# New places for a difference in quarters, for the ends of groups of statistics and for the last outputs

## Chip, cores, metric

One core of one Trainium2 chip. Times are device microseconds of that core, medians over executions. The changed kernel is compared with the kernel before on the same chip.

## The reference

Two layers of a compressed interaction network on x of 4096 rows, 32 fields, 16 numbers each (65536 sites), in float32:

```python
def _batchnorm(h, gamma, beta):
    mean = jnp.mean(h, axis=(0, 2), keepdims=True)
    var = jnp.var(h, axis=(0, 2), keepdims=True)
    return (h - mean) * jax.lax.rsqrt(var + EPS) * gamma[None, :, None] + beta[None, :, None]

def _cin_layer(out, x, W, b, gamma, beta):
    r, _, e = x.shape
    h = jnp.einsum('rne,rfe->rnfe', out, x).reshape(r, -1, e)
    h = jnp.einsum('rce,oc->roe', h, W) + b[None, :, None]
    return _batchnorm(h, gamma, beta)

h1 = _cin_layer(x, x, W1, b1, g1, beta1)             # 128 channels
out, direct1 = (h1[:, :64], h1[:, 64:])
direct2 = _cin_layer(out, x, W2, b2, g2, beta2)      # 64*32 products -> 128 channels
return jnp.concatenate([direct1, direct2], axis=1).sum(axis=-1)
```

## The kernel before

The second layer is 64 chunks of 512 columns. A chunk has four stages k = 0 to 3. In each, ScalarE makes two factors in PSUM, VectorE multiplies them with x into z ("zz", two products of 128x2048), and TensorE multiplies z with the weights. Three of the stages (k = 1, 2, 3) run a Strassen scheme, for which GpSimd adds parts of z into t. While a chunk's products are made, VectorE and ScalarE also put together the sums of the chunk before (`combine`, a generator; each `step()` runs one piece of it). The pieces that the change touches:

```python
def difference(part):                                     # 128x256, both inputs in SBUF
    cols = slice(part * T // 2, (part + 1) * T // 2)
    return nc.vector.tensor_tensor(xs[1][:, cols], xs[1][:, cols], xs[0][:, cols], ALU.subtract)

def combine(c, sums_):                                    # (cut)
    x62, x34, x57, x11 = sums_.banks                      # PSUM
    both = cpool.tile([P, T], FP, tag="both", name="both")
    act(both[low], x11[high])                             # ScalarE
    act(both[high], x11[low], bias=b2[low])
    if idle:
        dve(idle.pop(0))                                  # a quarter of the difference, if one is due
    yield
    add(both, both, x11)                                  # VectorE
    yield
    e = cpool.tile([P, 2, T], FP, tag="e", name="e")
    add(e[:, 0], both, x62)
    yield
    ...                                                   # u2, u3, u3_low, e[:, 1]
    dve(lambda: stats_x.add(c, e[:, 0]))                  # bn_stats; every 16th time also bn_aggr
    dve(lambda: stats_y.add(c, e[:, 1]))
    yield
    dve(lambda: nc.vector.tensor_reduce(d2[:, :, c, :], ..., AX.X, ALU.add))
    yield

for c in range(NC):                                       # (cut)
    ...
    if c % DIFF == 4:                                     # chunks 4, 20, 36
        idle += [lambda k=k: difference(k) for k in range(4)]
    for k, i in enumerate(STAGES):
        multiply(z[:, 0::3], f1, b)
        if k in (1, 2, 3): step()
        f2 = factor(raw[i], i, 1)
        if k == 1: step()
        multiply(z[:, 1:3], f2, bx)
        if k == 1: step()
        if k == 2: step()
        ...
        if k == 0: step(2)
        if k == 1: step()
        ...                                               # matmuls and, for k > 0, GpSimd's additions
```

After the loop: the rest of `combine`, the groups of statistics put together, scale and shift, one scaling each of dx and dy (128x2048), and four output transfers of 512 KB, each from 64 partitions.

## Time and profile before

| | before |
|---|---|
| median, lowest, highest of 4 runs | 2158.41, 2157.66, 2160.82 us |
| span of the profiled run | 2156.4 us |
| first to last matmul of the second layer | 1625.71 us |
| last matmul to the end | 23.12 us |

The last two rows are read from the view of two stretches of the profile. Columns: stretch, its length, busy time of TensorE, of its weight loads, VectorE, ScalarE, GpSimd (with counts), TensorE's clock, share and rate of the transfers.

```profile
507.62:2133.33 1625.71, 1606.69 (x7424) 527.15 (x7424) 1517.76 (x1038) 599.18 (x829) 1326.51 (x384) 1.00 0.70 164
2133.33:2156.45 23.12, 0.00 (x1) 0.00 (x0) 9.09 (x22) 3.51 (x4) 0.00 (x0) 0.61 0.41 91
```

TensorE is without work for about 19 us of the second layer (1625.71 - 1606.69), and for the 23 us behind it. The ends of matmuls are modelled in the profile, so stalls can also hide in TensorE's busy time.

### The profile page before, as it was taken

What the parts mean: (1) busy time and instruction counts of PE and PEld (TensorE: products, weight loads), DVE (VectorE), ACT (ScalarE), POOL (GpSimd) and SP (SyncE); (2) the same over time, 40 slices, a digit from 0 to 9 for tenths busy, and PEclk for the clock granted to TensorE, in tenths of its full rate; (3) what the DMA queues carried; (4) which work ended last, traced back from release to release, by engine and by line L of the source; (5) the groups of instructions that cost most, each with busy time, mean ns of one, the idle gap of its engine ahead of it and who ended that gap; (6) DMA issues with size and microseconds to landing.
All of it is one profiled execution on the core that took longest, in us unless ns stands there. A gap on an engine that the chain in (4) does not pass through costs nothing.

```text
span 2156.4 us, 23381 instructions
## 1 busy us (share of the span) xinstructions
PE 2095.2 (97%) x8716; PEld 732.2 (34%) x8716; DVE 1957.4 (91%) x1434; ACT 854.2 (40%) x1221; POOL 1328.3 (62%) x390
## 2 busy tenths in 40 slices
PE   7999999998999999999999999999999999999995
PEld 3344444443332333333223333332333333333331
DVE  7888889887999999899999999999999999999995
ACT  3455555554333333333333333333433333333332
POOL 0000000003877888877788888877888888788884
PEclk9999999999999999999999999999999999999998
DMA  9999999997767677776677777766676777766751
GB/s 348 343 345 329 338 348 362 344 339 188 173 155 167 169 184 173 174 173 160 156 167 184 167 173 170 179 162 156 157 176 165 173 172 173 167 165 163 172 125 40
DMA packets 111699, 440.64 MB, mean 204 GB/s; under 512 B 13024, under 2 KB 13024, under 8 KB 102880
## 3 DMA queue, kind: packets, MB, share of 16 engines
q1 hardware_dynamic: 104992, 416.33, 72.1%
q10 hardware_dynamic: 6592, 22.81, 2.9%
q8 instruction: 68, 1.11, 0.2%
q14 instruction: 47, 0.39, 0.1%
HBM read 417.07 MB, written 22.02 MB: 204 GB/s over the span
## 4 chain that ended last, share of the span: by engine, by line
PE 80%; POOL 11%; DVE 4%; issue 2%; DMA 2%; ACT 0%; SPq 0%; DVEq 0%; POOLq 0%
PE x L426 60%; PE ps L316 18%; POOL t L445 7%; POOL t L442 4%; DVE zz L401 2%; PE ps L314 1%; DVE z L304 1%; DMA b<-in_xb 1%; DVE e L396 0%; DMA a<-in_xa 0%; DMA x<-in_xb 0%; DMA r<-in_xr 0%; DVE direct L361 0%; DVE s_sb L252 0%; SPq L220 0%
## 5 line engine op out<-in xcount | busy, mean ns | idle before, releaser
L426 PE MATMUL x<-zz,w_sb 128*64 128x512 f32 x2560 | 969.0, 594 | 0.0
L442 POOL TENSOR_TENSOR t<-zz 128x1024 f32<-128x1024 f32 x192 | 456.7, 2378 | 787.2 <-DVE zz L401 787.1
L426 PE MATMUL x<-zz,s_sb 128*64 128x512 f32 x2048 | 924.9, 594 | 4.6 <-issue 4.6
L445 POOL TENSOR_TENSOR t<-zz,t 128x2048 f32<-128x2048 f32 x192 | 875.7, 4561 | 15.1
L426 PE MATMUL x<-t,s_sb 128*64 128x512 f32 x1536 | 700.9, 594 | 19.0 <-POOL t L445 19.0
L393 ACT ACTIVATE f<-a,keep 128x512 f32<-128x512 f32 x512 | 398.2, 778 | 637.9 <-DVE zz L401 635.1
L401 DVE TENSOR_TENSOR zz<-f,b 128x2048 f32<-128x2048 f32 x256 | 582.3, 2274 | 0.9 <-ACT f L393 0.8
L401 DVE TENSOR_TENSOR zz<-f,bx 128x2048 f32<-128x2048 f32 x256 | 582.5, 2275 | 0.0
L316 PE MATMUL ps<-z,w_sb 128*128 128x512 f32 x1024 | 450.5, 598 | 6.2 <-DVE z L304 6.2
L426 PEld LDWEIGHTS x<-zz,s_sb 128*64 128x64 f32 x2048 | 281.3, 137 | 371.9 <-issue 363.0
L426 PEld LDWEIGHTS x<-t,s_sb 128*64 128x64 f32 x1536 | 203.6, 137 | 475.3 <-issue 388.6
L426 PE MATMUL x<-t,w_sb 128*64 128x512 f32 x768 | 364.3, 597 | 0.0
L304 DVE TENSOR_TENSOR z<-a,b 128x2048 f32<-128x2048 f32 x128 | 292.6, 2286 | 58.3 <-DMA b<-in_xb 29.6
L426 PEld LDWEIGHTS x<-zz,w_sb 128*64 128x64 f32 x2560 | 301.6, 137 | 109.6 <-issue 107.6
L316 PEld LDWEIGHTS ps<-z,w_sb 128*128 128x128 f32 x1024 | 192.8, 191 | 262.6 <-issue 240.8
L426 PE MATMUL x<-zz,neg_sb 128*64 128x512 f32 x512 | 230.2, 592 | 0.0
L272 ACT ACTIVATE e<-ps,bn_sb 128x512 f32<-128x512 f32 x127 | 87.3, 687 | 245.2 <-PE ps L316 232.4
L396 DVE TENSOR_TENSOR both<-both,x 128x512 f32<-128x512 f32 x64 | 43.8, 685 | 105.2 <-ACT both L393 105.2
L393 ACT ACTIVATE u<-e,bn_sb 64x512 f32<-64x512 f32 x64 | 46.2, 722 | 216.3 <-DVE e L396 216.3
L426 PEld LDWEIGHTS x<-zz,neg_sb 128*64 128x64 f32 x512 | 70.2, 137 | 146.3 <-issue 146.3
L426 PEld LDWEIGHTS x<-t,w_sb 128*64 128x64 f32 x768 | 98.5, 137 | 0.0
L97 DVE BATCH_NORM_STATS2 stats<-e 128x6 f32<-128x512 f32 x127 | 87.1, 686 | 2.7 <-ACT e L272 2.7
(69 smaller groups left out, 870.5 us busy)
## 6 DMA issues: line engine op xcount, KB each, us to landing
a<-h SPq DMA_DIRECT2D x256, 512.0 KB, 5.5
b<-in_xb SPq DMA_DIRECT2D x128, 512.0 KB, 7.0
a<-in_xa SPq DMA_DIRECT2D x128, 512.0 KB, 5.9
b<-in_xb SPq DMA_DIRECT2D x64, 1024.0 KB, 7.1
bx<-in_xb SPq DMA_DIRECT2D x64, 512.0 KB, 6.1
bx<-x SPq DMA_DIRECT2D x64, 512.0 KB, 7.8
h<-kept ACTq DMA_DIRECT2D x64, 256.0 KB, 5.9
r<-in_xr SPq DMA_DIRECT2D x16, 512.0 KB, 7.5
```

Source lines behind the costliest of these rows:

```text
L97: done = nc.vector.bn_stats(self.stats[:, t % SG, :], h)
L272: nc.scalar.activation(e, ps, AF.Identity, bias=b1)
L304: nc.vector.tensor_tensor(z, a.rearrange("p (a t) -> p a t", a=2).unsqueeze(2).to_broadcast([P, 2, 2, T]), b.rearrange("p (b t) -> p b t", ...
L314: nc.tensor.matmul(ps, w1_sb[rows, 4 + s // 4, :], zr[rows, :], start=True, stop=False)
L316: nc.tensor.matmul(pss[t], w1_sb[:, m, :], z[:, m // 2, m % 2, :], start=False, stop=(m == 3))
L393: return queue("act", lambda: nc.scalar.activation(to, source, AF.Identity, **scale_bias))
L396: return dve(lambda: nc.vector.tensor_tensor(to, x, y, ALU.add))
L401: dve(lambda: nc.vector.tensor_tensor(z, a, b.rearrange("p (k q) t -> p k q t", k=2), ALU.mult))
L426: queue("pe", lambda: nc.tensor.matmul(self.of[x], w, b, start=start, stop=stop))
L442: queue("pool", lambda: nc.gpsimd.tensor_tensor(t2, t3, b11, ALU.add))
L445: queue("pool", lambda: nc.gpsimd.tensor_tensor(t[:, 1:3], z[:, 2:4], twice, ALU.subtract))
```

## The change

Its intent, as its edits show it: no VectorE instruction that could wait for GpSimd stands where GpSimd works. So the quarters move behind the next product, and the ends of the groups (which get two copies and, as groups now differ in size, scalings of the variance) go to the same place. The last group is small (4 in place of 16), so little is left for the end. The outputs are scaled and written in quarters, the first before the last reduction. The core of the diff:

```diff
-SG = 16
+SG = 20
+LAST = 4
@@ class Stats: add() no longer aggregates; instead
+        def aggregate(self):
+            size = self.sizes[self.group]            # 20, 20, 20, 4
+            group = self.groups[:, self.group]
+            stats = self.stats[:, :size].rearrange("p a b -> p (a b)")
+            done = nc.vector.bn_aggr(group[:, 1:3], stats)
+            if size != LAST:
+                done = nc.vector.tensor_scalar(group[:, 2:3], group[:, 2:3], size / LAST, None, ALU.mult)
+            ...
+    def swap_groups():
+        g = stats_x.group
+        stats_x.aggregate()
+        nc.vector.tensor_copy(groups2[low, 1, g], stats_x.groups[high, g])
+        return nc.vector.tensor_copy(groups2[high, 1, g], stats_x.groups[low, g])
@@ combine
-        if idle:
-            dve(idle.pop(0))
         yield
         add(both, both, x11)
         yield
         e = cpool.tile([P, 2, T], FP, tag="e", name="e")
+        if idle:
+            dve(idle.pop(0))
         add(e[:, 0], both, x62)
@@
+        if stats_x.ended():
+            ends = [swap_groups, stats_y.aggregate]
+            if c < NC - 1:
+                idle[:0] = [lambda: [end() for end in ends][-1]]
+            else:
+                for end in ends:
+                    dve(end)
@@ after the loop: the reduction is left for later, then
+    act(dy[:, :part], dy[:, :part], scale=ss2[:, 0:1], bias=ss2[:, 2:3])
+    write(nc.scalar, dy, 0, in_y)
+    scale(dx, 0, swapped)
+    write(nc.sync, dx, 0, in_x)
+    with tc.issue_after(lasts["dve"].ins):
+        step()                                       # the last reduction
+    scale(dx, 1, swapped)
+    write(nc.sync, dx, 1, in_x)
+    scale(dy, 1, ss2)
+    write(nc.scalar, dy, 1, in_y)
```

(Cut: the bookkeeping of groups, and `scale_shift` as a function of its own; the operations in it are the same.)

## The prediction

> **What bounds the kernel now.** I read the page first (busy shares, then the chain that ended last), then the waits, then the timelines of VectorE, GpSimd and TensorE side by side over single chunks.
>
> ```profile
> PE 2095.2 (97%) x8716; PEld 732.2 (34%) x8716; DVE 1957.4 (91%) x1434; ACT 854.2 (40%) x1221; POOL 1328.3 (62%) x390
> ...
> PE 80%; POOL 11%; DVE 4%; issue 2%; DMA 2%; ACT 0%; SPq 0%; DVEq 0%; POOLq 0%
> ```
>
> TensorE is busy 97% of the span and is 80% of the chain. GpSimd, busy only 62%, still holds 11% of the chain: somewhere TensorE waits for it. The kernel has two layers. The first ends near 500 us and the change hardly touches it. The second runs 64 chunks from 507.6 us to 2133.3 us. Each chunk has 7424/64 = 116 matmuls that run in pairs, 58 pairs, and in the timeline of TensorE a pair starts every 0.43 us: 24.85 us a chunk if nothing stalls.
>
> The starts of the addition into "both" (one a chunk, on VectorE) give the real periods. Most alternate between 24.89 and 25.0, mean 24.95. Three groups of chunks do not: periods 26.98, 26.94, 26.96, 26.99, 24.04, 25.84 for chunks 3 to 8, and nearly the same at chunks 19 to 24 and 35 to 40. Against 24.95 a chunk they cost 8.05, 7.98 and 8.04 us, together 24.1 us. These are the chunks in which a quarter of the "difference" stands in VectorE's order.
>
> ```profile
> L160 DVE TENSOR_TENSOR x<-x x16: 418/4146/4177, 70.5 to 1501.8; 128x256 f32<-128x256 f32 x16
> ```
>
> That is minimum, median and maximum in ns: 0.42 us in the first layer, where GpSimd does nothing, and about 4.15 us in the second. The timelines show why (VectorE, then GpSimd, then VectorE in a chunk without it):
>
> ```profile
> 1418.68 2.27 DVE L401 TENSOR_TENSOR zz<-f,bx 128x2048 f32<-128x2048 f32 x1
> 1420.88 4.17 DVE L160 TENSOR_TENSOR x<-x 128x256 f32<-128x256 f32 x1
> 1424.97 0.68 DVE L396 TENSOR_TENSOR both<-both,x 128x512 f32<-128x512 f32 x1
> ```
> ```profile
> 1420.23 4.53 POOL L445 TENSOR_TENSOR t<-zz,t 128x2048 f32<-128x2048 f32 x1
> 1430.78 2.38 POOL L442 TENSOR_TENSOR t<-zz 128x1024 f32<-128x1024 f32 x1 [6.02 <-DVE zz L401]
> ```
> ```profile
> 1373.08 0.69 DVE L396 TENSOR_TENSOR both<-both,x 128x512 f32<-128x512 f32 x1 [2.01 <-ACT both L393]
> ```
>
> The quarter is issued 0.65 us into GpSimd's last L445 of a chunk and ends 0.3 us after it (1420.23 + 4.53 = 1424.76). VectorE would have idled 2.01 us there anyway, waiting for ScalarE's "both"; the other 2.0 us push back both, two products, and so GpSimd's next L442. The waits name the victim: 85.5 us (85 times, some of each a gap that is always there) and 19.0 us of TensorE waiting for GpSimd's L445.
>
> ```profile
> PEld x L426 <- POOL t L445: 85.5, 85, 1.7
> PE x L426 <- POOL t L445: 19.0, 26, 0.8
> ```
>
> **What the Trainium skill says.** "SBUF — State Buffer", section "Who interferes with whom": a VectorE instruction with two SBUF inputs contends with a GpSimd instruction that reads SBUF, and whichever comes second blocks until the other is done. This trace agrees: 4.15 against 0.42 us. The same section says that an instruction with one SBUF input does not contend: the product L401 (its f is in PSUM) takes 2.27 us over a busy and over an idle GpSimd. It also lists copies and tensor_scalar as contending; the trace has one copy of 64x2 (L361) at 4.02 us while GpSimd works, and its twin at 0.17 us. Of transfers, the section "Door 1: The DMA port swizzle" gives a transfer from 64 partitions half the ports, and "Can I just issue two DMAs to hit both halves?" says two of them serialize. The last outputs agree: four transfers of 512 KB, 64 partitions each, have their packets from 2145.3 to 2155.1 us largely one after the other, 2.1 MB in 9.9 us.
>
> **The change part by part.**
>
> (1) The quarters move from before "both" to behind the next stage's first product (L401), before the addition into e. GpSimd is idle there: in the last chunk its L445 ends at 2106.45, that product ends at 2107.45 and the next L442 starts at 2110.39. So 1.0 us of margin before and 2.9 us of idle GpSimd after, and the quarter should take 0.42 us, some 0.34 of it net (neighbours overlap by 0.08). All three groups' 24.1 us of lock wait goes. In its place 0.34 us now lies on the path VectorE to GpSimd's first L442 to TensorE. How much slack has that path? Taking TensorE's first use of L445's result minus L445's end in a chunk without a quarter, from the timelines: about 1.9 us in the second stage, 1.0 in the third, 0.05 in the fourth, as each stage is 6.0 us of TensorE (14 pairs) and 6.95 of GpSimd. So there is none at a chunk's end, and a delay is a stall. But a chunk's L442 is released through both by the previous chunk's x11 sums, which come before the stall. The loop therefore spans two chunks (24.89 + 25.02 = 49.91 us), and of two delays of one size in a row the second falls into the time the first has bought. After a long stall the next chunk indeed shows 0.94 us of slack at its end. Four quarters in a row should cost 2 x 0.34 = 0.7 us.
>
> (2) The ends of a group of statistics. Before: two aggregations of 0.59 us in a stage with slack, and no chunk after one is longer. Now they go into the same slot as the quarters, at chunks 21, 41 and 61. An aggregation of 96 numbers takes 0.588 us and of 24 numbers 0.263, so 4.5 ns a number and 0.70 us for 120. Two of them, two scalings of 0.20 and two copies of 0.19 (durations 0.15 and 0.17 of such rows in the tail, with gaps): 2.2 us less some overlap, say 2.0 us. It is on the path with no slack, so each costs 2.0. At 41 and 61: 4.0. At 21 it stands among the quarters and hides one of them: 20 costs 0.34, 21 raises it to 2.0, 23 adds 0.34: 2.35. The loop: -24.1 + 0.7 + 2.35 + 0.7 + 4.0 = **-16.3 us**.
>
> (3) The tail after TensorE:
>
> ```profile
> 2136.31 0.69 DVE L97 BATCH_NORM_STATS2 statsx<-e 128x6 f32<-128x512 f32 x1
> 2137.04 0.59 DVE L102 BATCH_NORM_AGGREGATE groupsx<-statsx 128x2 f32<-128x96 f32 x1
> ...
> 2138.59 0.59 DVE L102 BATCH_NORM_AGGREGATE groupsy<-statsy 128x2 f32<-128x96 f32 x1
> 2139.10 1.16 DVE L490 TENSOR_REDUCE d<-e 128x64 f32<-128x1024 f32 x1
> 2140.17 0.16 DVE L552 COPY groups<-groupsy 128x12 f32<-128x12 f32 x1
> 2140.36 0.26 DVE L108 BATCH_NORM_AGGREGATE mv<-groups 128x2 f32<-128x24 f32 x1
> ```
>
> Last groups of 4 save 0.32 twice, the reduction behind the first scaling saves 1.08, the copy of y 0.19: mv starts 1.9 us earlier. The first scaling is a half: VectorE's 1.34 us becomes 0.7, so the first output is issued 1.9 + 0.65 = 2.55 us earlier. The second halves are issued about 1.8 us behind the first, while the first 1 MB still has 4.7 us to transfer, so they keep the transfers fed, and the end should move with the first issue: **-2.5 us**. Eight transfers instead of four may give some of it back.
>
> (4) Layer one ends with an aggregation of 24 numbers in place of 96: 0.58 - 0.26 = **-0.3 us**. The other ends there are of VectorE in a stage where transfers run at 99%: nothing. The additional memsets come in the first us.
>
> Sum: -16.3 - 2.5 - 0.3 = -19.1; 2159.06 - 19.1 = 2140.
>
> **The rivals.** (a) The lock moves with the quarter: if GpSimd still works when the slot comes, the wait returns. Against it: 1.0 us of margin. For it: the chunk behind an aggregation, where GpSimd runs 2 us late; there TensorE's own stall in the third stage delays both by about 1 us too, so margin remains. If it came back in a few chunks, 2145. (b) The loop does not forgive: every quarter costs its whole 0.34 us, 4.1 in place of 1.7, and the ends are longer (a copy that slips into GpSimd's time): 2143 to 2148. (c) The opposite: the ends overlap better, or the chunk that follows makes up for a part, as after the old groups (24.04 once): 2134 to 2137. (d) Transfers are the bound of the tail: with packets of 4 KB instead of 8 KB and eight issues the time after the last matmul stays: 2142.
>
> **Range and chances.** The first term is measured and sure, as the quarters can't wait where GpSimd is idle; the terms put in its place are estimates good to 3 us, the tail to 1.5 us, and the runs scatter by 1.5. 2134 to 2146 should hold it 8 times in 10. 2% is 43 us, more than all that the change touches (24 of quarters and 23 of tail): faster 0.02, slower 0.01, same 0.97.
>
> **What would show it.** In the changed profile the second layer's quarters take about 0.42 us, all periods of 27.0 are gone, the three group ends take about 2 us in front of an L401 and each is followed by a chunk period of about 26.9; mv starts some 5 us after the last matmul's end instead of 7.0, and the first output is issued 2.5 us nearer to it. It is wrong if a quarter still takes over 1 us, if the periods with a quarter are over 25.3, or if the time between the last matmul and the end has not shrunk by at least 1 us.

## The result, and the profile after

The changed kernel takes 2138.97 us (4 runs, 2137.44 to 2139.49) against 2158.41 us. The ratio of the fast runs is 0.9907 (95% interval 0.989 to 0.9924). The forecast was 2140 us, within a range of 2134 to 2146 us, and "the same within 2%": all held.

The page of the changed kernel, busy shares and chain:

```profile
PE 2091.2 (98%) x8716; PEld 733.8 (34%) x8716; DVE 1916.1 (90%) x1465; ACT 853.8 (40%) x1221; POOL 1328.5 (62%) x390
...
PE 83%; POOL 8%; DVE 4%; issue 2%; DMA 2%; ACT 1%; SPq 0%; DVEq 0%; POOLq 0%
```

TensorE's and GpSimd's work is what it was; VectorE lost 41 us of "busy" time that was waiting (12 quarters at 3.74 us are 45 us), and gained some instructions. The two stretches again, and the quarters (minimum, median, maximum in ns):

```profile
508.02:2116.86 1608.84, 1602.12 (x7424) 528.62 (x7424) 1475.55 (x1050) 599.46 (x829) 1326.67 (x384) 1.00 0.68 166
2116.86:2135.72 18.86, 0.00 (x0) 0.00 (x0) 9.35 (x23) 2.56 (x4) 0.00 (x0) 0.62 0.39 111
```
```profile
L184 DVE TENSOR_TENSOR x<-x x16: 414/416/424, 71.1 to 1488.2; 128x256 f32<-128x256 f32 x16
```

The second layer is 16.87 us shorter, the tail 4.26 us. No quarter waits any more. TensorE's waits for GpSimd's long addition (L481, formerly L445), of which 85.5 and 19.0 us stood before:

```profile
PEld x L462 <- POOL t L481: 58.5, 74, 1.7
PE x L462 <- POOL t L481: 6.5, 12, 0.8
```

A chunk with a quarter, VectorE first, then GpSimd:

```profile
634.51 2.28 DVE L437 TENSOR_TENSOR zz<-f,b 128x2048 f32<-128x2048 f32 x1
636.71 0.41 DVE L184 TENSOR_TENSOR x<-x 128x256 f32<-128x256 f32 x1
637.04 0.68 DVE L432 TENSOR_TENSOR e<-both,x 128x512 f32<-128x512 f32 x1
```
```profile
631.59 4.55 POOL L481 TENSOR_TENSOR t<-zz,t 128x2048 f32<-128x2048 f32 x1
640.07 2.38 POOL L478 TENSOR_TENSOR t<-zz 128x1024 f32<-128x1024 f32 x1 [3.92 <-DVE zz L437]
```

GpSimd is idle from 636.14 to 640.07, the quarter starts 0.57 us into that. The periods there are 25.35, 24.90, 25.36, 24.89: one delay of 0.34 us per pair of chunks (50.25 against 49.91 us), as forecast.

A group's end, VectorE, chunk 41:

```profile
1538.46 0.69 DVE L120 BATCH_NORM_AGGREGATE groupsx<-statsx 128x2 f32<-128x120 f32 x1
1539.06 0.64 DVE L120 BATCH_NORM_AGGREGATE groups<-statsy 128x2 f32<-128x120 f32 x1
...
1539.81 0.68 DVE L432 TENSOR_TENSOR e<-both,x 128x512 f32<-128x512 f32 x1
1540.52 0.16 DVE L409 COPY groups<-groupsx 64x3 f32<-64x3 f32 x1
...
1540.89 2.29 DVE L437 TENSOR_TENSOR zz<-f,bx 128x2048 f32<-128x2048 f32 x1
```

From the start of "both" (1535.65) to the second product went 5.24 us; without an end it is 3.40 us (1373.08 to 1376.48 before). So an end costs 1.84 us on the path. The two periods behind it are 25.87 and 25.84, 1.80 us above a normal pair.

The tail on VectorE:

```profile
2119.40 0.69 DVE L105 BATCH_NORM_STATS2 statsx<-e 128x6 f32<-128x512 f32 x1
...
2121.53 0.26 DVE L130 BATCH_NORM_AGGREGATE mv<-groups 128x2 f32<-128x24 f32 x1
...
2124.59 1.21 DVE L533 TENSOR_REDUCE d<-e 128x64 f32<-128x1024 f32 x1
```

mv starts 2.13 us behind statsx instead of 4.05, and the reduction stands behind the first scaling.

### The profile page after: what moved, and what is told of

Read it like the earlier page. It is cut to its first block, busy times and chain, and to the rows that moved or that the text cites. A ratio compares the mean times of both kernels' runs of the same rounds, so it can differ in the third digit from the quotient of the medians.

```text
span 2135.7 us, 23411 instructions
## 1 busy us (share of the span) xinstructions
PE 2091.2 (98%) x8716; PEld 733.8 (34%) x8716; DVE 1916.1 (90%) x1465; ACT 853.8 (40%) x1221; POOL 1328.5 (62%) x390
## 4 chain that ended last, share of the span: by engine, by line
PE 83%; POOL 8%; DVE 4%; issue 2%; DMA 2%; ACT 1%; SPq 0%; DVEq 0%; POOLq 0%
PE x L462 63%; PE ps L342 18%; POOL t L481 5%; POOL t L478 3%; DVE zz L437 2%; PE ps L340 1%; DVE z L330 1%; DMA b<-in_xb 1%; ACT both L429 0%; DMA x<-in_xb 0%; DMA a<-in_xa 0%; DMA r<-in_xr 0%; DVE e L432 0%; PE running L358 0%; DVE x L184 0%
## 5 line engine op out<-in xcount | busy, mean ns | idle before, releaser
L481 POOL TENSOR_TENSOR t<-zz,t 128x2048 f32<-128x2048 f32 x192 | 875.8, 4562 | 15.1
L429 ACT ACTIVATE both<-x 64x512 f32<-64x512 f32 x64 | 38.1, 595 | 138.6 <-PE x L462 138.6
```

The costliest lines, as they stand in the source:

```text
L429: return queue("act", lambda: nc.scalar.activation(to, source, AF.Identity, **scale_bias))
L481: queue("pool", lambda: nc.gpsimd.tensor_tensor(t[:, 1:3], z[:, 2:4], twice, ALU.subtract))
```

## The experiments

Ten more kernels ran. The first layer, in which they hardly differ, ends anywhere between 505.3 and 513.5 us in their profiles, and whole times scatter accordingly. The second layer's length scatters little (1608.84, 1608.73 and 1608.79 us in three kernels that differ only in the tail). So small differences are read from the second layer and the tail of the profile, and the times stand beside them.

| kernel | median of its fast runs, us | ratio to before, 95% | second layer, us | tail, us |
|---|---|---|---|---|
| before | 2158.41 | 1 | 1625.71 | 23.12 |
| changed | 2138.97 | 0.9907 (0.989 to 0.9924) | 1608.84 | 18.86 |
| e1 quarters only | 2140.65 | 0.99 (0.9886 to 0.9915) | 1603.95 | 23.11 |
| e2 one input (wrong on purpose) | 2137.4 | 0.9881 (0.9865 to 0.9898) | 1601.90 | 23.15 |
| e3 ends at once | 2141.37 | 0.9904 (0.9888 to 0.9919) | 1614.92 | 19.00 |
| e4 y low first | 2137.49 | 0.9888 (0.9869 to 0.9907) | 1608.73 | 19.03 |
| e5 ends on ScalarE | 2132.55 | 0.9867 (0.9851 to 0.9882) | 1603.83 | 18.94 |
| e6 quarters on GpSimd | 2134.6 | 0.9879 (0.9863 to 0.9896) | 1607.20 | 18.92 |
| e7 product first | 2125.73 | 0.9838 (0.9823 to 0.9852) | 1598.09 | 18.82 |
| e8 all three | 2125.04 | 0.9831 (0.9817 to 0.9846) | 1598.17 | 18.94 |
| e9 quarters late (one run, state unknown) | 2136.27 | none | 1608.79 | 20.30 |
| e10 wide outputs | 2144.93 | 0.9915 (0.9887 to 0.9943) | 1598.13 | 35.64 |

The experiments ran on other occasions than the result, on chip 13 (e1 to e4), 11 (e5 to e8) and 15 (e9, e10). Each ratio is to the kernel before on the same chip, whose medians there were 2162.65, 2160.76 and 2161.99 us. Medians of different groups are therefore not subtracted from each other below; every kernel that ran three rounds is "the same within 2%" as the kernel before.

### e1: the quarters alone

```diff
 # the kernel before
-        if idle:
-            dve(idle.pop(0))
         yield
         add(both, both, x11)
         yield
         e = cpool.tile([P, 2, T], FP, tag="e", name="e")
+        if idle:
+            dve(idle.pop(0))
```

> The kernel before with only the quarters of the difference moved behind the next product. Theory (the quarters waited for GpSimd's reads and pushed its next work back): each of the 12 takes 0.42 us, the three groups of periods of 27 us go (24.1 us), and in their place every second quarter costs 0.34 us, 2.0 us in all: 22 us less, 2136.4 us. Rival 1 (every quarter costs its whole 0.34 us, 4.1 in all): 2138.5. Rival 2 (the change's gain is mainly the tail and the ends): not under 2150.

Measured: 2140.65 against 2162.65 us on that chip, 22.0 us less; the 2136.4 us of the expectation was missed, as it started from the 2158.41 us of the result's own session. The second layer is 21.76 us shorter, each quarter takes 0.41 to 0.43 us, and periods of 25.32 to 25.35 us alternate with short ones. The tail is unchanged. The theory holds at 22 us, rival 2 falls; rival 1 is decided by e2. This one move gains more in the second layer than the whole change (16.87 us): the change gives 4.89 us back there, by the ends of the groups (1608.84 - 1603.95).

### e2: the old place, but one input

```diff
 # the kernel before; wrong result on purpose
-                idle += [lambda k=k: difference(k) for k in range(4)]
+                scrap = const.tile([P, 16], FP, tag="scrap", name="scrap")
+                def one_input(k):
+                    part = xs[1][:, k * 256 : (k + 1) * 256].rearrange("p (r e) -> p r e", e=EMB)
+                    return nc.vector.tensor_reduce(scrap, part, AX.X, ALU.add)
+                idle += [lambda k=k: one_input(k) for k in range(4)]
```

> Wrong result on purpose. The kernel before, and in the old place of the 12 quarters an instruction with one input in SBUF instead of two (a reduction over the same 256 columns). Theory (it is the second SBUF input that waits for GpSimd, not the place): it takes 0.4 us inside the 2 us for which VectorE waits there anyway, no period is over 25.2, and the time is 24 us less, 2134.4. Rival (the place in VectorE's order costs, whatever stands there): periods of 27 us stay, or of 25.3, and 2150 to 2158.

Measured: the second layer is 23.81 us shorter and no period but the very first is over 25.1 us. VectorE's timeline:

```profile
610.08 0.40 DVE L516 TENSOR_REDUCE scrap<-x 128x16 f32<-128x256 f32 x1
612.21 0.69 DVE L396 TENSOR_TENSOR both<-both,x 128x512 f32<-128x512 f32 x1 [1.73 <-ACT both L393]
```

An instruction of the same length and data, in the same place beside a working GpSimd, takes 0.40 us and disappears in the wait for ScalarE. So the place alone isn't what waited, and the second SBUF input is the reading that fits. (The stand-in is also another operation, a reduction with 16 results a row instead of 256; no run separates that.) The difference to e1, 1601.90 against 1603.95 us, is the price of the 12 quarters in their new place: 2.05 us, i.e. 0.34 us for every second one, not 4.1.

### e3: the ends of the groups at once

```diff
 # the changed kernel
-            if c < NC - 1:
-                idle[:0] = [lambda: [end() for end in ends][-1]]
-            else:
-                for end in ends:
-                    dve(end)
+            for end in ends:
+                dve(end)
```

> The changed kernel, with the ends of the statistics' groups where the kernel before had them: at once behind the last statistics, in a stage in which GpSimd works. Theory A (the ends cost their 1.84 us on the path in the slot they were moved to, and would be free in a stage with slack, as the aggregations were before): 5.5 us less than the changed kernel, about 2133.5. Theory B, the change's own reason (the copies and scalings would wait there for GpSimd): a copy or a scaling of more than 2 us in the trace, at chunks 20, 40 and 60, up to 4 us each, 2139 to 2150.

Measured: the second layer is 6.1 us longer than the changed kernel's, 1614.92 us. Theory A falls as stated; the change's own reason is right for the copies. VectorE, then GpSimd:

```profile
1020.79 0.15 DVE L122 TENSOR_SCALAR groupsx<-groupsx 128x1 f32<-128x1 f32 x1
1020.98 1.32 DVE L409 COPY groups<-groupsx 64x3 f32<-64x3 f32 x1
1022.32 0.16 DVE L410 COPY groups<-groupsx 64x3 f32<-64x3 f32 x1
```
```profile
1019.93 2.35 POOL L478 TENSOR_TENSOR t<-zz 128x1024 f32<-128x1024 f32 x1
1022.36 4.56 POOL L481 TENSOR_TENSOR t<-zz,t 128x2048 f32<-128x2048 f32 x1
```

The first copy ends when GpSimd's short addition does (1022.28), 1.16 us later than it need. The second slips between GpSimd's two instructions. It is the same at all three ends: 1.29 to 1.32 us for the first copy, 0.16 us for the second. The scaling of one column did not wait at all. Theory B was mis-sized too: the wait was under the 2 us named. With it the ends took 3.21 us, made GpSimd's next work 2.15 us late, and cost 3.8 to 4.0 us a pair of periods (26.14 + 27.56 at chunk 40, against 49.91).

### e5: the aggregations at once, the rest on ScalarE

```diff
 # the changed kernel (cut)
+            if c < NC - 1:
+                dve(stats_x.aggregate)                    # without the scaling
+                dve(stats_y.aggregate)
         yield                                             # and one step later:
+            for to, source, part in ((low, high, x), (high, low, x)):
+                act(groups2[to, 1, weigh, 0:2], part[source, 0:2])
+                act(groups2[to, 1, weigh, 2:3], part[source, 2:3], scale=SG / LAST)
+            act(y[:, 2:3], y[:, 2:3], scale=SG / LAST)
```

> The changed kernel with the groups' ends taken out of the slot: the two aggregations (one input, which did not wait in the run with the ends at once) stand at once behind the last statistics, where that run had 1.06 us of slack (3.21 us of ends made GpSimd's work 2.15 us late); the scalings and the copies go to ScalarE one step later. Theory (an end costs its 1.84 us in the slot because that slot is on the path; of 1.25 us in the earlier place only 0.2 us are too much): periods over 25.6 are gone, the second layer is 1604 us instead of 1608.8. Rival (the ends' cost is not the place: work on VectorE shows wherever it stands): 1608 to 1609.

Measured: 1603.83 us, 5.0 us less, and no period but the very first over 25.4. So an end's 1.84 us were paid because that slot is on the path: the two aggregations, 1.2 us of VectorE, cost nothing in the earlier place, against the rival. ScalarE takes 0.8 us for the five small pieces, and no period shows them. This is what e1 and the changed kernel together should give: e1's second layer, 1603.95 us, with the changed tail.

### e6: the quarters on GpSimd

```diff
 # the changed kernel
-idle += [lambda k=k: difference(k) for k in range(4)]                             # nc.vector
+pool_idle.extend(lambda k=k: difference(k, nc.gpsimd) for k in range(4))          # same slot, GpSimd's queue
```

> The changed kernel with the 12 quarters of the difference computed by GpSimd itself, first thing in its idle stretch of 3.9 us, instead of VectorE. Theory (the quarters' 0.34 us on VectorE are on the path, at 2.05 us in all): 0.6 to 1.2 us each on GpSimd, hidden; the periods of 25.3 at chunks 4, 6, 23, 36, 38 are gone and the second layer is 1606.8 us. Rival (GpSimd is the scarcer engine there, or VectorE and GpSimd block each other again): at or above 1608.8.

Measured: 1607.20 us, 1.6 us less, about as expected (1606.8). The rows of that difference on GpSimd:

```profile
L184 POOL TENSOR_TENSOR x<-x x12: 717/725/742, 608.0 to 1483.1; 128x256 f32<-128x256 f32 x12
```

0.73 us in an idle stretch of 3.9 us. The periods of 25.3 at the quarters are gone. One of 25.27 appears at chunk 33 that has none; I did not look for its cause.

### e7: the next product ahead of "both"

```diff
 # the changed kernel
             if k in (1, 2, 3):
-                step()
+                step(2 if k == 1 else 1)
 ...
             if k == 0:
-                step(2)
+                step(1)
```

> The changed kernel with the next product before the addition into both, in the 2 us in which VectorE waits for ScalarE. Theory (the loop over two chunks of 49.91 us, through both, two products and GpSimd, is what holds a chunk at 24.95 us where TensorE needs 24.85): the way from both to GpSimd's first work gets 0.7 us shorter (then the x62 sums end last), periods fall to 24.88, quarters and half of each end disappear into the slack, and the second layer is about 1597 us. Rival (TensorE alone sets 24.95, or another wait takes its place, such as the product's buffer): 1605 to 1612.

Measured: 1598.09 us (1597 expected) and 2125.73 us in all. VectorE in a chunk:

```profile
804.30 2.27 DVE L437 TENSOR_TENSOR zz<-f,b 128x2048 f32<-128x2048 f32 x1
807.00 0.69 DVE L432 TENSOR_TENSOR both<-both,x 128x512 f32<-128x512 f32 x1 [0.42 <-ACT both L429]
809.09 0.69 DVE L432 TENSOR_TENSOR e<-both,x 128x512 f32<-128x512 f32 x1 [1.41 <-PE x L462]
809.70 2.28 DVE L437 TENSOR_TENSOR zz<-f,bx 128x2048 f32<-128x2048 f32 x1
```

From both to the second product it is 2.70 us instead of 3.40, with e now waiting for TensorE's x62 sums. Every period but the first is 24.89 us, and TensorE's slack behind GpSimd's last addition is 0.65 us where it was 0.05. So the alternating 24.89 and 25.02 were the loop through both and GpSimd, not TensorE. The quarters here wait for GpSimd again (0.92 us in the median, as they now come earlier) and the ends stand in the same slot, and neither is seen in any period: on a path with slack they are free.

### e8: all three

> The changed kernel with the three edits of the last runs together. Theory: no period over 25.1 but for the first, the second layer 1596 us, the whole 12 to 13 us under the changed kernel, about 2126. If the three draw on the same slack it is no better than the product first alone.

The edits are those of e5, e6 and e7 together. Measured: 1598.17 us and 2125.04 us, not distinguishable from e7, so they draw on the same slack. A detail was wrong: three periods of 25.50 us appear, each followed by one of 24.29; a pair is 49.79 us, and nothing is lost. e7 alone, a change of two numbers, is the version to keep: its second layer is 10.75 us below the changed kernel's, at the same tail. (The 13.2 us between the medians compare two occasions.)

### e4 and e9: what shortened the transfers of the tail

```diff
 # e4: the changed kernel
-    in_y = ((high, 1, 0), (low, 0, ROWS // 2))
+    in_y = ((low, 0, ROWS // 2), (high, 1, 0))
 # e9: the changed kernel; reduction and whole scalings first, the same eight transfers behind them
-    step(8)
+    step(9)
 ...
+    nc.scalar.activation(dy, dy, AF.Identity, scale=ss2[:, 0:1], bias=ss2[:, 2:3])
+    nc.vector.tensor_scalar(dx, dx, swapped[:, 0:1], swapped[:, 2:3], ALU.mult, ALU.add)
+    for k in range(2):
+        write(nc.sync, dx, k, in_x)
+        write(nc.scalar, dy, k, in_y)
```

> The changed kernel with the two halves of y written in the order low, high, as x's are, so that both queues hold transfers of the same 64 partitions at one time. From the first issue of an output to the end went 12.4 us before and 11.0 after. Theory A (the change gained these 1.4 us because the queues' transfers now come from different halves of the partitions): 12.4 us again, the time 1.4 us longer, 2140.4. Theory B (more and smaller transfers alone did it): 11.0 us and no change, 2139.

> The changed kernel with the reduction and both whole scalings ahead of all outputs, as before, but the outputs in the same eight transfers of 256 KB. From the first issue of an output to the last landing went 11.4 us before and 9.9 after. Theory A (eight smaller transfers overlap better than four of 512 KB): again about 9.9 us, though the first issue is some 1.7 us later than in the changed kernel (0.54 us from the halved scaling and 1.2 us of reduction). Theory B (what counts is that the first half is issued before the second is ready, so the issuing is spread): 11.4 us.

Measured in e4: 11.2 us from the first issue to the end, against 11.0 in the changed kernel: the order of the halves does next to nothing, theory A falls. In e9: 9.84 us from the first issue to the last landing, as in the changed kernel (9.94) and not as before (11.41), although the first issue comes 1.5 us later behind the statistics. So eight transfers of 256 KB are through 1.5 us sooner than four of 512 KB, with the early start and without it; the early start is worth the rest (tail 18.86 against 20.30 us). e9 is a single run of unknown state, but its second layer (1608.79 us) and its clock (0.994) are those of fast runs. What in the eight does it isn't separated: each also has rows of half the length, and the trace's packets are 4 KB instead of 8 KB. Before, the packets pass in 9.88 us at 212 GB/s, in the changed kernel in 8.39 us at 250 GB/s, in e9 in 8.30 us at 253 GB/s.

### e10: outputs from 128 partitions

```diff
 # e7, y only (cut; y's halves in the order of e4)
-            to = out[KEEP + m * KEEP : KEEP + (m + 1) * KEEP, at : at + part]
-            engine.dma_start(to, d[half, k * part : (k + 1) * part])
+        to = bass.AP(out.tensor, out.offset + starts[0], [[starts[1] - starts[0], 2], [ROWS, KEEP], [1, part]])
+        engine.dma_start(to, d[:, k * part : (k + 1) * part])
```

> The kernel with the product first, and y written by two transfers of 512 KB from all 128 partitions instead of four of 256 KB from 64 (x's can't be, the two places in the output are in falling order). Theory (64 partitions hold a transfer to half of the ports): first issue to last landing 8 us or less instead of 9.8, the time about 2124. Rival (the writes are the limit, whatever the partitions): 9.8 us and 2125.7 as with the product first alone.

Measured: the tail is 35.64 us, 17 us longer. The theory, which takes up what the prediction cites on ports, isn't tested by this: the transfers ran on almost no engines. The stretch in which only y's transfers were left, columns as above:

```profile
2126.00:2141.00 15.00, 0.00 (x0) 0.00 (x0) 0.00 (x0) 0.00 (x0) 0.00 (x0) 0.50 0.13 52
```

A share of 0.13 of 16 engines is two engines, at 52 GB/s. The Trainium skill says why, in "DMA: Bandwidth & Descriptors", section "Why a DMA increments its semaphore by 16 and not by 1": the number of engines is the largest up to 16 that divides the slowest dimension of both sides, and I had made that dimension 2 on the output's side. The trace agrees with its two engines.

## Why the prediction was right

1. **The waits of the quarters, 24.1 us.** Right, and shown: 23.8 us without the second input (e2), and a quarter of 0.42 us wherever GpSimd is idle (e1 and the changed kernel).
2. **The quarters' price in the new place, 0.34 us for every second one.** Right: 2.05 us over three groups (e1 against e2), forecast 2.1. That the loop spans two chunks fits e7, which shortened it and so took the alternation away. The floor of a chunk is 24.89 us there, not the 24.85 of the prediction.
3. **The ends, 2.0 us each.** 1.84 us, as the scalings took 0.10 and 0.15 us instead of 0.20 each. The three together cost 4.89 us (changed kernel against e1); forecast were 5.65 (2.35 - 0.7 + 4.0). That is the direction of rival (c), by 0.8 us. The choice to book them as a loss, though the change means them as a gain, was right against e5 (5.0 us less). But leaving them as they stand in the old place would have been worse (e3): with the added copies the old place wasn't free any more.
   Sum of the second layer: -16.3 forecast, -16.87 measured.
4. **The tail, -2.5 us: the term that was mis-sized.** It became -4.26 us. mv earlier by 1.92 (forecast 1.9) and the first issue by another 0.53 (forecast 0.65) were right. Wrong was "the end should move with the first issue", with the fear that eight transfers give some back: first issue to last landing fell from 11.41 to 9.94 us, and e9, a single run, points to the eight smaller transfers themselves. Another 0.44 us came between the last matmul and statsx (2.98 to 2.54 us), where nothing was forecast. Of it 0.35 us are a stop of VectorE between the additions to u and to e (0.46 us idle before, 0.10 after); the profile doesn't show what it waited for, so the cause stays open. 0.1 us went back behind the last landing.
5. **Layer one, -0.3 us.** The aggregation took 0.26 us as forecast, but the first layer's end scatters by 8 us among the profiles (508.02 against 507.62 here), so the gain can't be seen. The 99% that the prediction gives for the transfers there is 96% in the profile before (100 to 480 us); TensorE is busy all of that stretch.

**The signs.** One of the prediction's signs of being wrong came up by the letter: three of the five lengthened periods with a quarter are over 25.3 us (25.32 to 25.36). The line was drawn too tight, since its own numbers give 25.02 + 0.34 = 25.36, and the pair of 50.25 us is as forecast. Another sign did not come: no end is followed by one period of about 26.9 us, but by two of 25.87 and 25.84. The prediction's own slacks give the reason, as an estimate that no run tests: of a delay of 1.84 us, the 1.0 us of slack in the third stage leaves 0.84 us to the next "both", and the rest falls behind it, at the end of the chunk.

**Luck.** That 2138.97 us lies within 1.1 us of 2140 is partly luck. The two stages gained 21.1 us in the profiles, 2.3 more than the 18.8 forecast for them, 1.8 of it in the tail; the medians, with the scatter of the first layer in them, differ by only 19.4.

Rival (a) did not happen in the changed kernel; it did in e7, where it cost nothing. Rival (b), each quarter at its whole price, is refuted by e1 against e2. Rival (d), transfers as the bound of the tail, held in part: from first issue to last landing they are over half of the tail (9.94 of 18.86 us), yet smaller ones were faster, not slower.

## What to carry to other kernels

Here a VectorE addition with two SBUF inputs (4.15 instead of 0.42 us) and a copy (1.3 instead of 0.16 us) waited beside a working GpSimd, and were better off in GpSimd's idle stretch. But here that stretch is the start of GpSimd's own path: what is put there is paid, an end with 1.84 us, unless the path has slack, as in e7. Before placing work, measure the slack of each place (the end of the releasing instruction against the start of the one that uses it), and first see whether a reordering can make slack: here two numbers in the order of steps were worth 10.75 us of the second layer, where the whole change had gained 16.87. Read small gains from the stage they belong to, as another stage's scatter can be larger than they are.

## What the Trainium skill lacked or had wrong

- "SBUF — State Buffer", "Who interferes with whom", lists tensor_scalar among the instructions that can contend, and refers to another page for the conditions of shape. I found none for a single column: a tensor_scalar of 128x1 did not wait (0.15 us in e3 while GpSimd worked), a copy of 64x3 behind it did (1.32 instead of 0.16 us).
- The same section has a blocked instruction wait for the other's end; it doesn't say that one can slip between two back-to-back GpSimd instructions. The second copy in e3 did, in a gap of 0.08 us, and so escaped 4.56 us.
- "GPSIMD Engine Reference": it times a two-input addition at 2048 columns and gives a rate from it, but no small one; 128x256 took 0.73 us there against 0.42 us on VectorE, and it was the cheaper place for the quarters, as GpSimd had an idle stretch (e6, 1.6 us).
- "SBUF — State Buffer", "The DMA setup-cost knee", advises the largest single transfer. For these last outputs, each from 64 partitions, eight of 256 KB on two queues landed 1.6 us sooner than four of 512 KB (9.84 against 11.41 us from first issue to last landing, e9 and before).
